# Prefix-attention layer on one core: reciprocals stored by two transfers and spread by four a block, TensorE's order in the loop fixed, picking and divisions queued behind the scan and the Gelu

## The chip, the cores and the metric

The kernel runs on one core of one Trainium2 chip. The metric is device time in microseconds (us): the median of the runs of one launch. Each launch takes the fp32 input `x` of shape (4, 128, 64, 64) and all weights from device memory and writes an output of `x`'s shape there.

## The reference

`x` holds four images of 128 channels and 4096 positions. Layer 0 normalises it by groups, runs three 1x1 convolutions with a PReLU, and adds a softmax attention over the 4096 positions. Layer 1 takes the positions as tokens `t` of 128 numbers and adds two things to them. The first is an attention with one query per head and a running softmax: at each token it is the mean over everything up to that token.

```python
kv = einsum('btd,ed->bte', x, W_kv).reshape(b, t, h, d, 2)   # 8 heads, d = 128
kv = silu(kv)
k, v = kv[..., 0], kv[..., 1]
s = einsum('hd,bthd->bth', q_proj, k)
m_A = cummax(s, axis=1)
exp_scores = exp(s - m_A)
u_A = cumsum(exp_scores, axis=1)
w_A = cumsum(exp_scores[..., None] * v, axis=1)
return (w_A / u_A[..., None]).mean(axis=2)
```

The second is a feed-forward part with 64 experts. Each expert picks its own eight tokens of an image, pools them by their probabilities, and its output goes back to the same tokens.

```python
logits = einsum('bsd,ed->bse', x, gate_w) + gate_b
probs = softmax(logits, axis=1)                      # over the 4096 tokens
vals, idx = top_k(probs.transpose(0, 2, 1), 8)
pooled = einsum('bked,bke->bed', gathered, topv)
h = gelu(einsum('ebd,edh->ebh', [pooled, 1], weight1))
out = einsum('ebh,eho->ebo', [h, 1], weight2)
outputs = zeros.at[flat_idx].add(out * topv)
```

Both parts read `t` normalised over its 128 numbers, and the second sees what the first has added.

## The kernel before

The whole of `t` stays on chip. Layer 0 (about the first 1500 us) ends before layer 1 begins, and the change does not touch it. Everything that follows is layer 1 (`layer1`), which has three parts: the loop over blocks, the tail with the experts, and the output.

**The loop.** The 16384 tokens are cut into 32 blocks of 512 (`NB`, `BLK`), eight (`NBLK`) to an image. Pass n of the loop (L982 on) finishes block n and prepares block n+1; the helpers it calls, each with its line, are these.

- `tokens` (L663): VectorE normalises the block's four chunks of 128 tokens (`xl`, L95). `turned` (L673): TensorE transposes them (`ltr`), ScalarE copies them out (`xt`).
- `keys` (L682): for each of eight heads one matmul `pk` (L687) into a PSUM tile and a Silu on ScalarE (`ks`, L689). The PSUM pool of these tiles has three buffers under the tag "kv"; `pk`, `pe`, `gtr`, `ctr`, `pv`, `pl`, `pp` and `ltr` all take their buffer from it in turn.
- `score` (L702): eight small matmuls give `ps`. `scan` (L712): VectorE copies it in two halves (`ss`), runs the maximum along the tokens (`mm`, L723), subtracts (L727); ScalarE takes the Exp (L728), GpSimd copies it into block order (`es`, L733); VectorE runs the sum (`rr`, L738), keeps the last value (L742), and takes the reciprocal 1/u (L743).
- `spread` (L746): 1/u has to reach all 128 partitions. SyncE stores `rr` to device memory (`rd`, L753) and loads it back, repeated 64 times (`rb`, L761).
- `weights` (L768): TensorE transposes `es` (`pe`, L772), ScalarE copies (`et`, L774), VectorE and GpSimd build `ew` (L779) and the masked `em` (L787). `weighted` (L794): VectorE multiplies `em` by `rb` (L796).
- `values` (L799): matmuls `pv` (L808) and Silus `v` (L812) on ScalarE. `totals` (L816): sums of the eight sub-blocks (`pt`, L824) and eight running sums on VectorE (`before`, L834). `outputs` (L836): TensorE combines all (`po`, L844 and L851), and VectorE adds it to `t` (L856).
- For the experts, a block or two behind: `gate_stats` (mean and variance, VectorE), `gate_norm` (L875: Sqrt on ScalarE, L90; reciprocal `grs` on VectorE, L91; the normalised `xg`, L95, on GpSimd), `gate_turn` (`gtr`, `xt2`), `gate_logits` (matmul `pl`, ScalarE's bias add `lg`, VectorE's best eight `ca`, L904).

**Picking.** For images 0 and 1 (p = 0) the picking is done inside the loop, in passes 18 to 26. `select` (L906) finds on VectorE the eight best of a whole image. Then `pick`, once a pass for eight passes: VectorE's match-replace marks the best in the block's logits (`left`, L930), ScalarE replaces the logits by their Exp (L933), and VectorE clears those that were not marked (L936). One pass later `pick_turn` (`ctr` L943, `ct` L946) and `pick_add` sum the chosen tokens. `divisors` (L971) takes one over the sum of the Exps, once. For images 2 and 3 (p = 1) the same is done in the tail.

**What sets the order.** A planner sorts each engine's instructions by a priority that follows the program's order. `tc.issue_after(x)` puts what is issued in its block behind instruction x on the same engine. In the loop it stands around `weighted`, `gate_norm` and `pick`. [...] SyncE's queue holds the stores and loads of `spread`.

**The tail** (L1032 on) makes the gate of the last two blocks, picks for p = 1, and runs 16 groups of four experts: `first` (`ph` L1099, copy `hr` L1104), `turn` (transposes `htr` L1111, bias add L1115, Gelu L1120), `second` (L1127), `back` (transposing `t` for the output, L1141). One block of Exps is scaled by the divisor per group (`probs`, L1156). Then the experts' outputs (`eo`, L1164) are put back by matmuls (`sct`) and the output is written.

Functions with a second prefix ("g_") belong to a branch that is not executed.

Of the kernel before, what the change touches and what calls it, by code (L numbers as in the profile page):

```python
# [8 lines left out]
F32 = mybir.dt.float32  # L9
AF = mybir.ActivationFunctionType  # L10
# [8 lines left out]
def conv_attn_hybrid_kernel(  # L19
# [22 lines left out]
    nc = tc.nc  # L42
    B, C, N = x.shape
    R = w1t.shape[1]
    NH = qt.shape[1]
# [3 lines left out]
    NCH = N // P  # L49
    BLK = 512  # L50
    NBLK = N // BLK
# [575 lines left out]
    QG = 4  # L627
# [9 lines left out]
    def layer1(pre, ready):  # L637

        with ExitStack() as kept, ExitStack() as l1:
# [72 lines left out]
            def scan(n, pss):  # L712

                k = n % NBLK
                ss = sb.tile([P, BLK], F32, tag="ss", name=f"{pre}ss_{n}", bufs=1)
                for q in range(NPAIR):
                    half = bass.ts(q, BLK // NPAIR)
                    nc.vector.tensor_copy(
                        ss[:, half].rearrange("h (u s j) -> h s u j", u=2, s=2),
                        pss[:, half].rearrange("h (s u j) -> h s u j", u=2, s=2),  # L720
                    )
                mm = sb.tile([P, BLK], F32, tag="mm", name=f"{pre}mm_{n}", bufs=1)
                nc.vector.tensor_tensor_scan(  # L723
                    out=mm, data0=ss, data1=ss, op0=ALU.max, op1=ALU.max,
                    initial=state[:, 0:1] if k else LOWEST,
                )
                nc.vector.tensor_sub(ss, ss, mm)  # L727
                exp = nc.scalar.activation(ss, ss, AF.Exp).ins  # L728
                nc.gpsimd.tensor_copy(state[:, 0:1], mm[:, BLK - 1 : BLK])  # L729
                es = sb.tile([P, BLK], F32, tag="es", name=f"{pre}es_{n}")  # L730
                for q in range(NPAIR):
                    half = bass.ts(q, BLK // NPAIR)
                    nc.gpsimd.tensor_copy(  # L733
                        es[:, half].rearrange("h (s u j) -> h s u j", u=2, s=2),
                        ss[:, half].rearrange("h (u s j) -> h s u j", u=2, s=2),
                    )
                rr = sb.tile([P, BLK], F32, tag="rr", name=f"{pre}rr_{n}")
                nc.vector.tensor_tensor_scan(  # L738
                    out=rr, data0=ones.to_broadcast([P, BLK]), data1=ss,
                    op0=ALU.mult, op1=ALU.add, initial=state[:, 1:2] if k else 0.0,  # L740
                )
                nc.vector.tensor_copy(state[:, 1:2], rr[:, BLK - 1 : BLK])  # L742
                nc.vector.reciprocal(rr, rr)  # L743
                return es, rr, exp

            def spread(n, rr):  # L746

                rd = dram.tile([2, NPAIR, 2, NH, H2], F32, tag="rd", name=f"{pre}rd_{n}")
                by_row = rr.rearrange("(g w) (q u s j) -> w u g q s j", g=QG, q=NPAIR, u=2, s=2)
                for r in range(NR):  # L750
                    for u in range(2):
                        for q in range(NPAIR):
                            nc.sync.dma_start(  # L753
                                out=rd[u, q, :, r * QG : (r + 1) * QG, :].rearrange("s g j -> g s j"),
                                in_=by_row[r, u][:, q],
                            )
                rbs = []
                for q in range(NPAIR):
                    rb = sb.tile([P, 2, NH, H2], F32, tag="rb", name=f"{pre}rb_{n}_{q}")
                    for u in range(2):  # L760
                        nc.sync.dma_start(  # L761
                            out=rb[u * H2 : (u + 1) * H2],
                            in_=rd[u, q].unsqueeze(0).to_broadcast([H2, 2, NH, H2]),
                        )
                    rbs.append(rb)
                return rbs
# [173 lines left out]
            def pick_turn(p, k, ps):  # L940
                ptr = ps.tile([P, CPB, P], F32, tag="kv", name=f"{pre}ctr_{p}_{k}")
                for c in range(CPB):
                    nc.tensor.transpose(ptr[:, c, :], lgs[p][:, bass.ts(k * CPB + c, P)], ident)  # L943
                ct = gp.tile([P, CPB, 2, E], F32, tag="ct", name=f"{pre}ct_{p}_{k}", bufs=2)
                rs = rs1[:, bass.ts(p, 2 * NCH)].rearrange("t (z i) -> t i z", z=2)
                nc.vector.tensor_mul(  # L946
                    ct, ptr.rearrange("t c (z e) -> t c z e", z=2),
                    rs[:, bass.ts(k, CPB), :].unsqueeze(3).to_broadcast([P, CPB, 2, E]),
                )
                cts[p, k] = ct  # L950

            def pick_sum(p, k, pp, start, stop):
                for c in range(CPB):
# [21 lines left out]
            if not ready:  # L975
                for at in range(B * NCH):
                    chunk_stats(gp, mv1[:, at, :], at, f"{pre}st1_{at}")
                roots(rs1, mv1)
            xt = {n: turned(n, tokens(n)) for n in range(2)}
            made = scan(0, score(0, keys(0, xt[0], range(NH))))  # L980
            rbs = spread(0, made[1])
            for n in range(NB):  # L982
                more = n + 1 < NB
                if more:
                    ks = keys(n + 1, xt[n + 1], range(NH // 2))
                if n >= 1:
                    gate_stats(n - 1)
                if n + 2 < NB:
                    xls = tokens(n + 2)
                    xl_last = xls.pop()  # L990
                es, rr, _ = made
                ems = weights(n, es)
                if n >= 2:
                    gate_turn(n - 2, ps_kv)
                if more:
                    ks += keys(n + 1, xt[n + 1], range(NH // 2, NH))
                with tc.issue_after(xl_last):
                    aas = weighted(ems, rbs)
                k0 = n - (B // 2 * NBLK + 2)
                if 1 <= k0 <= NBLK:  # L1000
                    pick_turn(0, k0 - 1, ps_kv)
                vs, last = values(n, xt[n])
                if n >= 2:
                    best = gate_logits(n - 2, ps_kv)
                if 1 <= k0 <= NBLK:
                    pick_add(0, k0 - 1)
                with tc.issue_after(last):
                    if n >= 1:
                        gate_norm(n - 1, nc.gpsimd)
                    if n == 0 and ready:  # L1010
                        roots(rs1[:, bass.ts(B - 1, NCH)], mv1[:, bass.ts(B - 1, NCH), :])
                if n + 2 < NB:
                    xt[n + 2] = turned(n + 2, xls)
                totals(n, vs)
                if more:
                    made = scan(n + 1, score(n + 1, ks))
                    rbs = spread(n + 1, made[1])
                    last = made[2]
                with tc.issue_after(last):
                    if k0 == 0:  # L1020
                        select(0)
                    if 0 <= k0 < NBLK:
                        pick(0, k0)
                    if k0 == NBLK:
                        divisors(0)
                outputs(n, rr, aas, vs)
                if n >= 2:
                    best()
                if n == 0 and ready:
                    test_rows(gp, ps_kv)  # L1030

            l1.close()  # L1032
            pool = opener(l1, pre)
# [28 lines left out]

            gate_stats(NB - 1)
            gate_norm(NB - 1, nc.vector)
            for n in (NB - 2, NB - 1):
                gate_turn(n, ps_a)
                gate_logits(n, ps_a)()
            select(1)
            pp = ps_p.tile([P, C + 1], F32, tag="pp", name=f"{pre}pp_1")
            for k in range(NBLK + 1):  # L1070
# [36 lines left out]
            def turn(g, hr):  # L1107

                ptr = ps_a.tile([P, FC, QG, QW], F32, tag="kv", name=f"{pre}htr_{g}")
                for c in range(FC):  # L1110
                    nc.tensor.transpose(  # L1111
                        ptr[:, c].rearrange("p u b -> p (u b)"), hr[:, bass.ts(c, P)], ident
                    )
                hs = fs.tile([P, FC, QG, QW], F32, tag="hs", name=f"{pre}hs_{g}")
                nc.vector.tensor_tensor(  # L1115
                    hs, ptr,
                    fb1s[:, bass.ts(g, QG), :].rearrange("p u c -> p c u")
                    .unsqueeze(3).to_broadcast([P, FC, QG, QW]), ALU.add,
                )
                nc.scalar.activation(hs, hs, AF.Gelu)  # L1120
                return hs

            def second(g, hs):
                po = ps_p.tile([P, C], F32, tag="po", name=f"{pre}po2_{g}")
# [21 lines left out]

            hr = first(0)
            for g in range(EG):
                hs = turn(g, hr)
                if g + 1 < EG:  # L1150
                    hr = first(g + 1)
                for n in range(g * NB // EG, (g + 1) * NB // EG):
                    back(n)
                p, k = g // NBLK, g % NBLK
                probs = lgs[p][:, bass.ts(k, BLK)]
                nc.scalar.activation(probs, probs, AF.Copy, scale=rden[:, p : p + 1])  # L1156
                second(g, hs)
            eo = []
            for p in range(B // 2):
# [94 lines left out]
```

## Time and profile before

| | us |
|---|---|
| median of 3 runs | 2545.86 |
| lowest and highest | 2544.01, 2548.97 |
| the profiled execution | 2545.14 |
| its span, first to last instruction | 2543.4 |
| layer 1's loop, first scan to last scan | 842.1 |
| tail and output, from the last scan | 187.7 |

The loop's first scan (L723) starts at 1513.60 and its last at 2355.73, both of the span. The page cuts the span into 40 slices of 63.6 us; the loop lies in slices 24 to 37, where TensorE is busy for 90% or more in all but the first:

```
PE   5899999999999999999999989999999999999787
DVE  6677777777776777766666665655656656665624
ACT  2344434444344444444444445565655665666431
POOL 0000000000000000000000002333333333333200
PEclk9999999999999999999999999999999999999898
DMA  3100110000100000000000002111121111112485
```

Each digit is a busy share in tenths. PEclk is the clock granted to TensorE, in tenths of full speed. Groups of instructions that the change touches, with busy time and the mean length of one:

```
L743 DVE RECIPROCAL rr<-rr 128x512 f32<-128x512 f32 x32 | 107.2, 3351 | 0.8
L796 DVE TENSOR_TENSOR em<-em,rb 128x1024 f32<-128x1024 f32 x64 | 78.4, 1226 | 242.4 <-DMA rb<-rd 242.3
L728 ACT ACT_TABLE_LOAD x32 | 41.1, 1283 | 209.3 <-DVE ss L727 209.3
L689 ACT ACTIVATE ks<-pk 128x512 f32<-128x512 f32 x256 | 146.6, 598 | 55.4 <-PE pk L687 55.0
rd<-rr SPq DMA_DIRECT2D x256, 2.0 KB
rb<-rd SPq DMA_DIRECT2D x128, 256.0 KB
```

Behind the bar stand the busy time in us, the mean of one in ns, and the engine's idle time just before these instructions with what ended most of it. The last two are transfers: how many, and the size of each. A table load brings another function (Exp, Silu, Sqrt) into ScalarE.

### The profile page before, as it was taken

The page shows a single profiled execution, that of the slowest core. Times are in us where ns is not written, and L with a number is a line of the kernel's source. Part 1 is how long each engine was busy: PE and PEld are TensorE (multiplying, and loading weights), DVE is VectorE, ACT ScalarE, POOL GpSimd, SP SyncE. Part 2 cuts the span into 40 slices and gives each one's busy share as a digit, 9 for nine tenths or more (in the row PEclk, how much of TensorE's full clock was granted, in tenths as well). Part 3 has the DMA queues.
Part 4 walks back from the last instruction along what each step waited for, and adds up shares of the span by engine and source line. Part 5 has one row for each costly group of instructions (what it writes and reads, how often), then busy time and mean ns, then how long its engine had stood idle before and what let it go on. Part 6 is the DMA issues. An engine that isn't in the chain of part 4 may idle for free.

```text
span 2543.4 us, 45698 instructions
## 1 busy us (share of the span) xinstructions
PE 2406.8 (95%) x19348; PEld 1592.4 (63%) x19348; DVE 1662.0 (65%) x2644; ACT 1182.3 (46%) x1557; POOL 311.6 (12%) x374
## 2 busy tenths in 40 slices
PE   5899999999999999999999989999999999999787
PEld 3567767677677677776777755555555555555543
DVE  6677777777776777766666665655656656665624
ACT  2344434444344444444444445565655665666431
POOL 0000000000000000000000002333333333333200
PEclk9999999999999999999999999999999999999898
DMA  3100110000100000000000002111121111112485
GB/s 96 56 17 12 27 50 9 17 11 24 50 13 5 17 22 17 17 9 9 5 5 9 5 1 52 36 42 46 35 52 36 35 48 40 36 35 52 159 332 210
DMA packets 49063, 111.06 MB, mean 44 GB/s; under 512 B 10960, under 2 KB 19792, under 8 KB 48720
## 3 DMA queue, kind: packets, MB, share of 16 engines
q1 hardware_dynamic: 47552, 107.78, 14.3%
q8 instruction: 153, 2.51, 0.4%
q14 instruction: 62, 0.51, 0.1%
q10 hardware_dynamic: 1296, 0.26, 0.1%
HBM read 86.38 MB, written 8.91 MB: 37 GB/s over the span
## 4 chain that ended last, share of the span: by engine, by line
PE 61%; DVE 19%; DMA 7%; SPq 6%; ACT 3%; issue 2%; ACTq 0%; DVEq 0%; POOL 0%
PE av L494 34%; PE sc L470 17%; DMA rb<-rd 6%; SPq L753 4%; DVE rr L743 4%; DVE before L834 2%; SPq L761 2%; DVE rr L738 2%; ACT L728 2%; DVE mm L723 1%; DVE em L796 1%; PE pa L437 1%; PE ph L1099 1%; PE pd L519 1%; DVE xl L95 1%
## 5 line engine op out<-in xcount | busy, mean ns | idle before, releaser
L494 PE MATMUL av<-pr,am 64*128 64x512 f32 x4096 | 1190.1, 592 | 5.5 <-DVE o L505 5.5
L474 ACT ACTIVATE pr<-sc 128x1024 f32<-128x1024 f32 x512 | 523.9, 1023 | 705.6 <-PE sc L470 695.1
L494 PEld LDWEIGHTS av<-pr,am 64*128 64x128 f32 x4096 | 679.2, 188 | 258.4 <-issue 59.4
L481 DVE TENSOR_TENSOR acc<-acc,pr 128x1024 f32<-128x1024 f32 x480 | 585.4, 1220 | 332.8 <-ACT pr L474 320.8
L470 PE MATMUL sc<-e,e 64*128 64x512 f32 x2048 | 737.1, 594 | 0.0
L470 PEld LDWEIGHTS sc<-e,e 64*128 64x128 f32 x2048 | 351.9, 188 | 102.3 <-issue 29.0
L687 PE MATMUL pk<-xt,wks 128*128 128x512 f32 x512 | 250.3, 624 | 45.2 <-ACT ks L689 40.1
L796 DVE TENSOR_TENSOR em<-em,rb 128x1024 f32<-128x1024 f32 x64 | 78.4, 1226 | 242.4 <-DMA rb<-rd 242.3
L808 PE MATMUL pv<-wvs,xt 128*128 128x512 f32 x512 | 226.0, 594 | 0.0
L687 PEld LDWEIGHTS pk<-xt,wks 128*128 128x128 f32 x512 | 91.9, 194 | 157.4 <-issue 76.8
L812 ACT ACTIVATE v<-pv 128x512 f32<-128x512 f32 x256 | 152.7, 597 | 68.5 <-PE pv L808 68.4
L689 ACT ACTIVATE ks<-pk 128x512 f32<-128x512 f32 x256 | 146.6, 598 | 55.4 <-PE pk L687 55.0
L808 PEld LDWEIGHTS pv<-wvs,xt 128*128 128x128 f32 x512 | 97.1, 191 | 118.7 <-issue 116.3
L728 ACT ACT_TABLE_LOAD x32 | 41.1, 1283 | 209.3 <-DVE ss L727 209.3
L95 POOL TENSOR_SCALAR xg<-t,gmv,grs 128x128 f32<-128x128 f32 x124 | 98.8, 809 | 258.2 <-DVE grs L91 211.9
L695 POOL MEMSET ew<- 128x1024 f32 x1 | 1.0, 951 | 1051.7 <-PE pa L437 1051.7
L844 PEld LDWEIGHTS po<-v,em 64*64 64x64 f32 x4096 | 111.4, 133 | 28.8 <-DVE before L834 10.9
L844 PE MATMUL po<-v,em 64*64 64x128 f32 x4096 | 119.4, 271 | 2.3 <-DVE em L796 2.3
L787 POOL TENSOR_TENSOR em<-et,mask 128x1024 f32<-128x1024 f32 x64 | 120.3, 1901 | 6.4 <-ACT et L774 6.4
L527 DVE RECIPROCAL den<-den 128x512 f32<-128x512 f32 x32 | 107.3, 3353 | 1.1
L743 DVE RECIPROCAL rr<-rr 128x512 f32<-128x512 f32 x32 | 107.2, 3351 | 0.8
L729 POOL COPY state<-mm 128x1 f32<-128x1 f32 x32 | 20.7, 646 | 508.5 <-DVE mm L723 508.3
(164 smaller groups left out, 2275.4 us busy)
## 6 DMA issues: line engine op xcount, KB each, us to landing
rb<-rd SPq DMA_DIRECT2D x128, 256.0 KB
fw<-in_fw_dram SPq DMA_DIRECT2D x64, 512.0 KB
x<-in_x_dram SPq DMA_DIRECT2D x16, 512.0 KB
xr<-in_x_dram SPq DMA_DIRECT2D x32, 256.0 KB
e<-ee SPq DMA_DIRECT2D x64, 128.0 KB
out_dram<-t SPq DMA_DIRECT2D x16, 512.0 KB
e<-ee SPq DMA_DIRECT2D x64, 64.0 KB
rd<-rr SPq DMA_DIRECT2D x256, 2.0 KB
```

Source lines behind the costliest of these rows:

```text
L95: i = engine.tensor_scalar(out=dst, in0=t[:, chunk, :], scalar1=mean, scalar2=rs, op0=ALU.subtract, op1=ALU.mult)
L470: nc.tensor.matmul(sc[:, u, :], e2[halves[u], p, :], e1[halves[u], :], start=True, stop=True)
L474: nc.scalar.activation(pr, sc, AF.Exp)
L481: nc.vector.tensor_add(acc, acc, pr)
L494: nc.tensor.matmul(av, am[h, j, :], pr[h, u, :], start=(j == 0), stop=(j == NCH - 1))
L687: nc.tensor.matmul(pk, wks[:, h, :], xt, start=True, stop=True)
L689: nc.scalar.activation(ks, pk, AF.Silu)
L743: nc.vector.reciprocal(rr, rr)
L787: nc.gpsimd.tensor_tensor(em, eq.unsqueeze(2).to_broadcast([P, 2 * NH, H2]), mask.unsqueeze(1).to_broadcast([P, 2 * NH, H2]), ALU.mult,)
L808: nc.tensor.matmul(pv.rearrange("p h d -> p (h d)"), xt[:, bass.ts(2 * q + s, P)], wvs[:, bass.ts(m, BLK)], start=True, stop=True,)
L812: last = nc.scalar.activation(v[:, bass.ts(m, HPB), :], pv, AF.Silu).ins
L844: nc.tensor.matmul(po[s * H2 : (s + 1) * H2, u, q, :], aas[q][half, s, h, :], vs[2 * q + s][half, h, :], start=(q == 0 and h == 0), stop=F ...
```

## The change

The change has four parts.

1. `spread` stores a block's 1/u in another layout by two transfers of 8 KB, instead of eight of 2 KB. The four loads of 256 KB read this layout. `scan` now also returns its reciprocal instruction.
2. The loop stands in a function that runs with TensorE's order fixed to the program's order. A few calls change place with it: in pass 0 the second half of `keys` comes before `weights`, and the norm, turn and logits of block 30 come into the last pass, with `xg` on VectorE instead of GpSimd.
3. `select`, `pick` and `divisors` are put behind the scan's Exp on ScalarE and behind the scan's reciprocal on VectorE, where they were behind the Exp alone. `weighted`, which was behind the last `xl` of `tokens`, comes behind `pick_turn` in the passes that have one, and has no such edge in the others.
4. In the tail, each group's scaling of `probs` comes behind that group's Gelu on ScalarE.

Of the loop the diff shows the new lines alone; those that they replace are L979 to L1030 above.

```diff
                     op0=ALU.mult, op1=ALU.add, initial=state[:, 1:2] if k else 0.0,
                 )
                 nc.vector.tensor_copy(state[:, 1:2], rr[:, BLK - 1 : BLK])
-                nc.vector.reciprocal(rr, rr)
-                return es, rr, exp
+                inverse = nc.vector.reciprocal(rr, rr).ins
+                return es, rr, (exp, inverse)
             def spread(n, rr):
-                rd = dram.tile([2, NPAIR, 2, NH, H2], F32, tag="rd", name=f"{pre}rd_{n}")
-                by_row = rr.rearrange("(g w) (q u s j) -> w u g q s j", g=QG, q=NPAIR, u=2, s=2)
+                rd = dram.tile([NPAIR, 2, 2, NH, H2], F32, tag="rd", name=f"{pre}rd_{n}")
+                by_row = rr.rearrange("(g w) (c j) -> w g c j", g=QG, j=H2)
                 for r in range(NR):
-                    for u in range(2):
-                        for q in range(NPAIR):
-                            nc.sync.dma_start(
-                                out=rd[u, q, :, r * QG : (r + 1) * QG, :].rearrange("s g j -> g s j"),
-                                in_=by_row[r, u][:, q],
-                            )
+                    nc.sync.dma_start(
+                        out=rd.rearrange("q u s (r g) j -> r g (q u s) j", r=NR)[r], in_=by_row[r]
+                    )
                 rbs = []
                 for q in range(NPAIR):
                     rb = sb.tile([P, 2, NH, H2], F32, tag="rb", name=f"{pre}rb_{n}_{q}")
                     for u in range(2):
                         nc.sync.dma_start(
                             out=rb[u * H2 : (u + 1) * H2],
-                            in_=rd[u, q].unsqueeze(0).to_broadcast([H2, 2, NH, H2]),
+                            in_=rd[q, u].unsqueeze(0).to_broadcast([H2, 2, NH, H2]),
                         )
                     rbs.append(rb)
                 return rbs
...
                     nc.tensor.transpose(ptr[:, c, :], lgs[p][:, bass.ts(k * CPB + c, P)], ident)
                 ct = gp.tile([P, CPB, 2, E], F32, tag="ct", name=f"{pre}ct_{p}_{k}", bufs=2)
                 rs = rs1[:, bass.ts(p, 2 * NCH)].rearrange("t (z i) -> t i z", z=2)
-                nc.vector.tensor_mul(
+                i = nc.vector.tensor_mul(
                     ct, ptr.rearrange("t c (z e) -> t c z e", z=2),
                     rs[:, bass.ts(k, CPB), :].unsqueeze(3).to_broadcast([P, CPB, 2, E]),
                 )
                 cts[p, k] = ct
+                return i.ins
             def pick_sum(p, k, pp, start, stop):
                 for c in range(CPB):
...
                 for at in range(B * NCH):
                     chunk_stats(gp, mv1[:, at, :], at, f"{pre}st1_{at}")
                 roots(rs1, mv1)
...
+            def loop():
+                xt = {n: turned(n, tokens(n)) for n in range(2)}
+                made = scan(0, score(0, keys(0, xt[0], range(NH))))
+                rbs = spread(0, made[1])
+                for n in range(NB):
+                    more = n + 1 < NB
+                    if more:
+                        ks = keys(n + 1, xt[n + 1], range(NH // 2))
+                    if n >= 1:
+                        gate_stats(n - 1)
+                    if not more:
+                        gate_norm(n - 1, nc.vector)
+                    if n + 2 < NB:
+                        xls = tokens(n + 2)
+                    if n == 0:
+                        ks += keys(n + 1, xt[n + 1], range(NH // 2, NH))
+                    es, rr, _ = made
+                    ems = weights(n, es)
+                    if n >= 2:
+                        gate_turn(n - 2, ps_kv)
+                    if more and n > 0:
+                        ks += keys(n + 1, xt[n + 1], range(NH // 2, NH))
+                    k0 = n - (B // 2 * NBLK + 2)
+                    if 1 <= k0 <= NBLK:
+                        with tc.issue_after(pick_turn(0, k0 - 1, ps_kv)):
+                            aas = weighted(ems, rbs)
+                    else:
+                        aas = weighted(ems, rbs)
+                    vs, last = values(n, xt[n])
+                    if n >= 2:
+                        best = gate_logits(n - 2, ps_kv)
+                    if not more:
+                        gate_turn(n - 1, ps_kv)
+                    if 1 <= k0 <= NBLK:
+                        pick_add(0, k0 - 1)
+                    with tc.issue_after(last):
+                        if n >= 1 and more:
+                            gate_norm(n - 1, nc.gpsimd)
+                        if n == 0 and ready:
+                            roots(rs1[:, bass.ts(B - 1, NCH)], mv1[:, bass.ts(B - 1, NCH), :])
+                    if n + 2 < NB:
+                        xt[n + 2] = turned(n + 2, xls)
+                    totals(n, vs)
+                    if not more:
+                        best()
+                        best = gate_logits(n - 1, ps_kv)
+                    if more:
+                        made = scan(n + 1, score(n + 1, ks))
+                        rbs = spread(n + 1, made[1])
+                        with tc.issue_after(made[2][0]), tc.issue_after(made[2][1]):
+                            if k0 == 0:
+                                select(0)
+                            if 0 <= k0 < NBLK:
+                                pick(0, k0)
+                            if k0 == NBLK:
+                                divisors(0)
+                    outputs(n, rr, aas, vs)
+                    if n >= 2:
+                        best()
+                    if n == 0 and ready:
+                        test_rows(gp, ps_kv)
+            with tc.manual_schedule(engines={mybir.EngineType.PE}):
+                loop()
             l1.close()
             pool = opener(l1, pre)
...
             gate_stats(NB - 1)
             gate_norm(NB - 1, nc.vector)
-            for n in (NB - 2, NB - 1):
-                gate_turn(n, ps_a)
-                gate_logits(n, ps_a)()
+            gate_turn(NB - 1, ps_a)
+            gate_logits(NB - 1, ps_a)()
             select(1)
             pp = ps_p.tile([P, C + 1], F32, tag="pp", name=f"{pre}pp_1")
             for k in range(NBLK + 1):
...
                     fb1s[:, bass.ts(g, QG), :].rearrange("p u c -> p c u")
                     .unsqueeze(3).to_broadcast([P, FC, QG, QW]), ALU.add,
                 )
-                nc.scalar.activation(hs, hs, AF.Gelu)
-                return hs
+                return hs, nc.scalar.activation(hs, hs, AF.Gelu).ins
             def second(g, hs):
                 po = ps_p.tile([P, C], F32, tag="po", name=f"{pre}po2_{g}")
...
             hr = first(0)
             for g in range(EG):
-                hs = turn(g, hr)
+                hs, gelu = turn(g, hr)
                 if g + 1 < EG:
                     hr = first(g + 1)
                 for n in range(g * NB // EG, (g + 1) * NB // EG):
                     back(n)
                 p, k = g // NBLK, g % NBLK
                 probs = lgs[p][:, bass.ts(k, BLK)]
-                nc.scalar.activation(probs, probs, AF.Copy, scale=rden[:, p : p + 1])
+                with tc.issue_after(gelu):
+                    nc.scalar.activation(probs, probs, AF.Copy, scale=rden[:, p : p + 1])
                 second(g, hs)
             eo = []
             for p in range(B // 2):
```

## The prediction

> **What bounds the kernel now.** I read first the page's busy shares and the chain that ended last, then the windows view of layer 1 cut at the scan's starts, then TensorE's waits in those windows, and last single turns in the timeline.
>
> ```profile
> PE 2406.8 (95%) x19348; PEld 1592.4 (63%) x19348; DVE 1662.0 (65%) x2644; ACT 1182.3 (46%) x1557; POOL 311.6 (12%) x374
> ...
> PE av L494 34%; PE sc L470 17%; DMA rb<-rd 6%; SPq L753 4%; DVE rr L743 4%; DVE before L834 2%; SPq L761 2%; DVE rr L738 2%; ACT L728 2%; DVE mm L723 1%; DVE em L796 1%; PE pa L437 1%; PE ph L1099 1%; PE pd L519 1%; DVE xl L95 1%
> ```
>
> TensorE is busy for 95% of the span, but `av` and `sc` are layer 0, which the change leaves alone. Layer 1's part of the chain is another thing: stores (L753), loads (L761), `rb<-rd`, reciprocal. So cut it into turns; turn n runs from the scan L723 of block n to that of block n+1.
>
> ```profile
> 1567.62:1967.56 399.94, 377.04 (x5077) 215.13 (x5071) 235.82 (x526) 239.22 (x375) 144.27 (x167) 1.00 0.17 42
> ...
> 2022.96:2251.00 228.04, 218.76 (x2964) 127.95 (x2960) 143.66 (x319) 137.54 (x224) 77.67 (x89) 0.99 0.16 39
> ```
>
> ```profile
> PE pk L687 <- ACT ks L689: 22.5, 14, 2.2
> ```
>
> Columns of the windows: window, length, busy of PE, PEld, DVE, ACT, POOL, then PEclk, DMA share, GB/s. Turns 2 to 16 last 399.94/15 = 26.66 each and TensorE works 377.04/15 = 25.14 of it. The 1.5 between them is one wait a turn (the waits view of turns 2 to 16: 22.5 in all, 14 waits, 2.2 the longest), put down to ScalarE; ScalarE is late because of the chain of one turn:
>
> ```profile
> 1806.99 1.21 DVE mm L723
> ...
> 1812.69 3.35 DVE rr L743
> ...
> 1816.60 0.04 SPq L753
> ...
> 1820.01 0.50 SPq L753
> ...
> 1820.62 0.50 SPq L761
> ...
> 1822.48 5.49 DMA rb<-rd
> ...
> 1828.05 1.23 DVE em L796
> ...
> 1834.10 1.21 DVE mm L723
> ```
>
> From the scan's start: reciprocal ends at +9.13; eight stores issue until 1820.52 and four loads from 1820.62, last byte at 1827.97, 11.93 after the reciprocal; `em` ends at 1829.27; 4.75 of VectorE's small work (`xl`, `grs`, `ca`, six `before` sums, the copies of `ss`) leads to the next scan. VectorE, kept by rb, turns the next tokens late, and ScalarE and TensorE wait for that. So plain turns hang on the spread, by 1.5.
>
> The pick turns 19 to 26 (second window) are TensorE's: 228.04 long, and its waits there add to 0.5 (turn 19), 4.8 (20 to 25) and 4.0 (26). Lengths: 28.01, six of 27.79, 33.29. TensorE's own need is about 26.99.
>
> [...] 8 KB of `eo` landed 1.27 after its issue. [...] after 5.0 of idle at 1541 to 1546:
>
> ```profile
> 1546.00:1547.00 1.00, 0.39 (x1) 0.39 (x2) 1.00 (x5) 0.00 (x0) 0.00 (x0) 0.50 0.00 0
> ...
> 1551.00:1552.00 1.00, 1.00 (x4) 0.48 (x3) 0.48 (x2) 0.23 (x2) 0.44 (x1) 0.50 0.13 51
> ...
> 1553.00:1554.00 1.00, 1.00 (x4) 0.46 (x3) 0.50 (x1) 0.74 (x2) 1.00 (x2) 1.00 1.03 234
> ```
>
> [...] Turn 26 of before shows it: the scaling of L1156 waits 3.88 for a VectorE division, the Silu behind it waits with it, and TensorE loses 3.09:
>
> ```profile
> 2229.21 0.72 ACT L1156 ACTIVATE lg<-lg,rden 128x512 f32<-128x512 f32 x1 [3.88 <-DVE rden L973]
> ...
> 2229.84 0.58 ACT L689 ACTIVATE ks<-pk 128x512 f32<-128x512 f32 x1
> ...
> 2230.47 5.40 PE L687 MATMUL pk<-xt,wks 128*128 128x512 f32 x8 [3.09 <-ACT ks L689]
> ```
>
> **Part 1, the spread.** Eight stores of 2 KB become two of 8 KB; the four loads and their bytes stay. The stores' issue, 8 x 0.55, becomes 2 x 0.52 = 1.05. But the loads now follow their stores so closely that they must wait for the landing: before, none waited (the load of the last store was issued 1.25 after it). I take 1.4; bounds 1.25 (below it a wait would have shown) [...]. The loads themselves took 7.35 from first issue to last byte, at 215 to 240 GB/s, and that stays. So 1.05 + 1.4 + 7.35 = 9.8 instead of 11.93: 2.1 saved [...]. The chain's 26.66 falls to 24.6, under TensorE's 25.14; TensorE is late next, and the gain is cut to 1.5 less some leftover wait, 0.2. Plain turn 25.34.
> Turns 2 to 16: 15 x 25.34 - 399.94 = -19.8. Turn 17: 29.05 to 25.34, -3.7. Turn 18: 26.35, -1.0. Turns 27 to 30: 104.73 against TensorE's 100.8 and 0.4 left over, -3.5.
>
> **Part 2, the picking.** In the instruction order of the changed program, VectorE's match-replace (L930) now stands right behind the reciprocal, and ScalarE's queue in a pick turn reads: Exp of `ss`, Silu table load, `ks_0`, Exp table load, Exp of `lg`, Silu table load, `ks_1` to `ks_7`. Before it read: Exp of `ss`, Exp of `lg`, one Silu load, `ks_0` and on. Exp of `lg` overwrites what the match-replace reads, so it waits for it, and seven Silus queue behind the wait. The prices stand in one pick turn of before:
>
> ```profile
> 2082.68 0.71 ACT L933 ACTIVATE lg<-lg,ng 128x512 f32<-128x512 f32 x1
> ...
> 2083.50 1.28 ACT L689 ACT_TABLE_LOAD   x1
> ...
> 2084.80 1.57 ACT L689 ACTIVATE ks<-pk 128x512 f32<-128x512 f32 x3
> ...
> 2085.16 0.68 DVE L930 MATCH_REPLACE8 left<-ca,lg 128x512 f32<-128x512 f32 x1
> ```
>
> Reciprocal at +9.13 (plain turn: nothing of the picking is ahead of it now), match-replace 0.68 and gaps: +9.90; Exp of `lg` from +9.94; table load and start of `ks_1` 2.12 later (2082.68 to 2084.80): +12.06, ended +12.61. TensorE, whose order is fixed, has behind the last `ps` (1.26 before the scan) `po` with L851 4.67, four `pk` 3.54: ready at +6.95 for `pe`. The PSUM pool "kv" has three buffers, and the one `pe` wants is freed by `ks_1`. Stall: 12.66 - 6.95 = 5.7, with the restart 5.86. The first pick has `select`'s small VectorE work, about 4.1, ahead of its match-replace, but lets `ks_1` and `ks_2` through first: 8.2.
> A wait of that length also drops the clock: before shows 0.50 for one or two windows of 3.4 us behind idles of 3 to 5 us. 3.1 to 6.5 us of work at half speed lose 1.6 to 3.3; I take 2.4 (from 0 to 3.3). A pick turn: 26.99 + 5.86 + 2.4 = 35.25; turn 19: 37.6.
> Turn 19: +9.6. Turns 20 to 25: 6 x 35.25 - 166.74 = +44.8. Turn 26: 33.29 to 35.25, +2.0; it loses the eight scalings and their 3.09 wait, and takes the pick's stall.
> Nothing hides this stall: TensorE is the bound of these turns, and spread's 2 us of slack is no help to it.
>
> **Part 3, the rest.** The scalings of L1156 go behind each group's Gelu, where ScalarE is idle for most of a group's 5.95: nothing. TensorE's fixed order is nearly the one it had; the first turns lose a wait of `pe` for `es`: -1.4. Norm, turn and logits of block 30 move into the last pass: its Sqrt table load and the Silu load after it stand in ScalarE's queue among the `v` activations, and hold TensorE for about 3.2, `po` gets its rb 2.1 earlier, and a Sqrt load of 1.28 comes onto the tail's path; with small waits +3.5 (0 to 6). In the tail one `gtr` and `pl` go, covered there.
>
> **Sum.** -19.8 - 3.7 - 1.0 + 9.6 + 44.8 + 2.0 - 3.5 - 1.4 + 3.5 = +30.5. The profiled execution took 2545.14 (span 2543.4), 0.7 under the runs' median of 2545.86. Predicted 2576. With x for what a pick turn has over TensorE's 26.99, the sum is 8x - 38: it breaks even at x = 4.7; mine is 8.55. Without the clock's share x is 6.15, still slower. About 5 us, 0.2%, is what a measurement can tell from no change.
>
> **Rivals.**
> A, main, 0.70: as above, 2576; 2562 to 2590 from the clock's 1.6 to 3.3, the last pass and the landing.
> B, 0.12: the spread gains a third of that, because [...] the loads are bound by their megabyte. Plain turns 26.3: 17 x 0.96 more, 2592. For: the loads fill 5.5 of 11.9. Against: the 4.4 of issue that goes stood on the chain in full.
> C, 0.09: stall without a clock drop (x = 6.15): 8 x 6.15 - 38 = +11, 2557. [...] Against: turn 26 of before, where 3.09 of idle was followed by 3.2 at 0.50.
> D, the other side, 0.09: the match-replace is ready when ScalarE gets to its Exp, so that only ScalarE's own two loads and Exp count, 2 x 1.28 + 0.71 less TensorE's slack: x = 3.0[...]; -14, 2532. It decides below x = 4.7, that is if `ks_1` ends 1.2 earlier against TensorE than I have it and the clock holds. For: all of +6.95 is pieced together from other turns. Against: the 3.35 reciprocal stands ahead of the match-replace in VectorE's order, and in before the match-replace was ready only because it stood ahead.
>
> Slower 0.88, within 0.2% 0.02, faster 0.10. The range reaches from C to B: 2555 to 2594.
>
> **What will show it.** TensorE waits for ScalarE's `ks` before `pe`, 5 to 6 us each in seven turns and about 8 in turn 19, with PEclk of 0.50 behind each; ScalarE's L933 Exp waits for the match-replace, with a table load on both sides. Scan to scan: 25.3 in turns 2 to 16, 35 in 20 to 25. Two stores a block[...], and a chain through layer 1 that runs over TensorE. I am wrong if pick turns stay under 31.7, or if plain turns stay above 26.

## The result, and the profile after

| | before | after |
|---|---|---|
| median, us (4 runs each) | 2545.81 | 2558.73 |
| lowest and highest | 2544.01, 2548.97 | 2557.49, 2560.27 |
| profiled execution's span | 2543.4 | 2555.8 |

The changed kernel is slower by 12.9 us: ratio 1.005, 95% interval 1.0032 to 1.0067. Slower was forecast, but 30 us were expected, more than twice as much. In the spans the difference is 12.4.

The page of the changed kernel, busy shares and chain:

```profile
PE 2412.5 (94%) x19348; PEld 1598.9 (63%) x19348; DVE 1677.5 (66%) x2648; ACT 1206.8 (47%) x1575; POOL 310.0 (12%) x370
...
PE 84%; DVE 9%; ACT 3%; DMA 2%; issue 1%; SPq 0%; ACTq 0%; DVEq 0%
```

Before, TensorE had 61% of that chain, DMA 7% and SyncE's queue 6%. The spread has all but left the path: outside the pick turns the chain of the loop now runs over TensorE, and `rb<-rd` has 1.6% of it in turns 2 to 16, where it had 19.4% before. The windows view shows turns 2 to 16 (the first line) and the pick turns 19 to 26 (the second):

```profile
1563.27:1935.68 372.41, 372.35 (x5035) 212.94 (x5029) 236.58 (x526) 239.41 (x375) 144.47 (x167) 1.00 0.19 45
...
1985.45:2262.09 276.64, 231.68 (x2964) 136.98 (x2956) 158.76 (x330) 155.38 (x232) 79.96 (x89) 0.90 0.14 32
```

The first stretch took 399.94 before and takes 372.41, with TensorE busy in all of it. The second took 228.04 and takes 276.64. The waits view of TensorE in the second stretch has almost all of what came on top (us in all, how many, longest):

```profile
PE pe L769 <- ACT ks L689: 38.0, 7, 5.5
PE pk L687 <- ACT ks L689: 7.0, 1, 7.0
```

TensorE stood idle for 45.0 us. One such turn in the timeline (turn 21, scan at 2056.62):

```profile
2061.96 0.60 ACT L689 ACTIVATE ks<-pk 128x512 f32<-128x512 f32 x1
...
2062.40 3.35 DVE L743 RECIPROCAL rr<-rr 128x512 f32<-128x512 f32 x1
2062.57 1.28 ACT L930 ACT_TABLE_LOAD   x1
...
2065.69 0.67 DVE L927 MATCH_REPLACE8 left<-ca,lg 128x512 f32<-128x512 f32 x1
...
2066.40 0.72 ACT L930 ACTIVATE lg<-lg,ng 128x512 f32<-128x512 f32 x1 [2.54 <-DVE left L927]
...
2067.23 1.28 ACT L689 ACT_TABLE_LOAD   x1
...
2068.52 1.57 ACT L689 ACTIVATE ks<-pk 128x512 f32<-128x512 f32 x3
2069.26 1.09 PE L769 MATMUL pe<-ident,es 128*128 128x128 f32 x4 [5.47 <-ACT ks L689]
```

Read it from below. `pe` has stood 5.47 for a buffer that `ks_1` frees; `ks_1` stood behind a table load, the Exp of `lg`, and the table load ahead of that; the Exp stood 2.54 for the match-replace, which came behind the 3.35 of the reciprocal. The windows view over the same turn shows what became of TensorE's clock (last column but two):

```profile
2066.00:2067.00 1.00, 0.00 (x0) 0.00 (x0) 1.00 (x3) 0.60 (x1) 0.00 (x0) 0.95 0.00 0
2068.00:2069.00 1.00, 0.00 (x0) 0.00 (x0) 0.80 (x4) 0.99 (x2) 0.56 (x1) 0.50 0.00 0
2072.00:2073.00 1.00, 1.00 (x3) 0.48 (x2) 0.61 (x1) 0.05 (x1) 1.00 (x2) 0.50 1.11 246
2073.00:2074.00 1.00, 1.00 (x2) 0.32 (x2) 0.00 (x0) 0.55 (x1) 1.00 (x1) 0.64 0.82 180
2074.00:2075.00 1.00, 1.00 (x4) 0.44 (x3) 0.00 (x0) 0.60 (x1) 0.43 (x1) 1.00 0.05 8
```

The clock was at half from about 2066.9 to 2073.7, and TensorE's first 4.4 us of work fall into it. Where the 12.4 of the spans come from, with the prediction's terms beside them:

| stretch | predicted | measured |
|---|---|---|
| to the first scan, and turns 0 and 1 | -1.4 | -4.4 |
| turns 2 to 16 | -19.8 | -27.5 |
| turns 17 and 18 | -4.7 | -5.6 |
| turn 19 | +9.6 | +8.3 |
| turns 20 to 25 | +44.8 | +39.4 |
| turn 26 | +2.0 | +0.9 |
| turns 27 to 30 | -3.5 | -4.9 |
| from the last scan on | +3.5 | +6.2 |
| sum | +30.5 | +12.4 |

Of the first row, 1.2 lies ahead of the first scan, mostly in layer 0, which the change leaves alone. The first scan starts anywhere from 1511.1 to 1513.8 in the thirteen kernels, so that part says nothing of the change. Of turn 17's gain of 4.1, the spread brings 1.6 (27.46 in e1 below). The other 2.5 comes with the pick's edge: with the spread alone `select` and the first match-replace stood at 1959 to 1962, ahead of the next scan at 1964.68; in the changed kernel they stand in turn 19.

### The profile page after: what moved, and what is told of

Read it like the earlier page. It is cut to its first block, busy times and chain, and to the rows that moved or that the text cites. A ratio compares the mean times of both kernels' runs of the same rounds, so it can differ in the third digit from the quotient of the medians.

```text
span 2555.8 us, 45522 instructions
## 1 busy us (share of the span) xinstructions
PE 2412.5 (94%) x19348; PEld 1598.9 (63%) x19348; DVE 1677.5 (66%) x2648; ACT 1206.8 (47%) x1575; POOL 310.0 (12%) x370
## 4 chain that ended last, share of the span: by engine, by line
PE 84%; DVE 9%; ACT 3%; DMA 2%; issue 1%; SPq 0%; ACTq 0%; DVEq 0%
PE av L494 33%; PE sc L470 17%; PE pv L805 8%; PE pk L687 8%; PE po L841 3%; PE pt L821 2%; DVE rr L743 2%; PE ps L706 1%; PE pa L437 1%; PE ph L1108 1%; PE pd L519 1%; DVE before L831 1%; PE pp L955 1%; PE pe L415 1%; PE pl L896 1%
```

## The experiments

Each run's ratio is against the kernel before, measured beside it (its median moved between 2545.1 and 2546.9). The changed kernel was timed in the first group alone, so a difference from it carries an uncertainty of 1 to 2 us.

**The spread alone (e1_spread).** On the kernel before, `spread` as in the change and nothing else; TensorE's order stays as it was.

```diff
-                    for u in range(2):
-                        for q in range(NPAIR):
-                            nc.sync.dma_start(
-                                out=rd[u, q, :, r * QG : (r + 1) * QG, :].rearrange("s g j -> g s j"),
-                                in_=by_row[r, u][:, q],
-                            )
+                    nc.sync.dma_start(
+                        out=rd.rearrange("q u s (r g) j -> r g (q u s) j", r=NR)[r], in_=by_row[r]
+                    )
```

> The kernel before with the new spread alone (two stores of 8 KB a block, loads from the new layout); TensorE's order is the one of before. Theory 'spread' (the store issue stood on the chain, and TensorE is next): plain turns fall from 26.66 to 24.8 to 25.1, the pick turns 20 to 25 from 27.8 to about 27.2, turn 26 stays near 33; in all some -33 to -36 us, about 2511. Rival 'order' (the fixed order of TensorE brought the plain turns down to 24.8): plain turns stay at 25.3 or more, and at most -25 us. Rival 'bytes' (the loads bound it): under -8 us.

2504.29, ratio 0.9827 (0.981 to 0.9844): 42.5 us faster, more than either theory gave. The windows view, turns 2 to 16:

```profile
1564.94:1937.22 372.28, 372.25 (x5032) 212.89 (x5026) 236.39 (x526) 239.40 (x375) 143.46 (x167) 1.00 0.19 45
```

That is 24.82 a turn with TensorE full, the same as in the changed kernel, though TensorE's order is that of before. So the gain of the plain turns is the spread's, and 'order' falls. Turns 0 and 1 become 2.8 shorter as well, and turns 20 to 25 fall from 27.79 to about 27.36.

**The pick as before (e2_pick_old).** The changed kernel with one edge less.

```diff
-                        with tc.issue_after(made[2][0]), tc.issue_after(made[2][1]):
+                        with tc.issue_after(made[2][0]):
```

> The changed kernel with the pick behind the scan's Exp alone again, so that VectorE has the match-replace ahead of the reciprocal and ScalarE the Exp of the logits directly behind the scan's Exp, as before the change. Theory 'queue' (the pick's place makes the stall): TensorE's waits before pe, 45 us in turns 19 to 26, go, and PEclk stays at 1.0 there; pick turns fall from 34.3 to about 27; 50 to 58 us faster than the changed kernel, 2501 to 2509. Rival 'fixed order' (the stall comes from TensorE's order being fixed, with pe where the scan's chain is latest): the waits before pe stay over 3 us a turn and the time over 2530.

2501.57, ratio 0.9816 (0.9798 to 0.9833): 57.2 us below the changed kernel. Turns 19 to 26:

```profile
1989.52:2208.34 218.82, 215.81 (x2968) 127.30 (x2963) 144.29 (x322) 133.34 (x216) 77.77 (x89) 1.00 0.17 41
```

The clock is 1.00 throughout and TensorE's waits are down to 3.0 in all. This also takes the loss of 57.8 in these turns apart. 42.0 of it is more standing. The other 15.9, or 2.0 a turn, is busy time: the same work takes 215.81 here and 231.68 in the changed kernel. That is put down to half clock, and a separate count gives the same size: in the changed kernel TensorE is busy for 34.6 us, over all stretches of these turns with its clock at half, and half of that is 17.3. The moved edge of `weighted` has no run of its own; e1 has the old one and e2 the new one, and turns 20 to 25 last 27.35 in both.

**The pick's edge alone (e3_pick_only).** On the kernel before: `pick` behind the reciprocal too, eight stores, planner's order.

```diff
-                with tc.issue_after(last):
+                with tc.issue_after(last[0]), tc.issue_after(last[1]):
                     if k0 == 0:
                         select(0)
```

> The kernel before with the pick behind the reciprocal alone; spread with its eight stores, TensorE's order left to the planner. Theory 'queue': ScalarE's queue is that of the changed kernel in the pick turns (two more table loads, the Exp behind the match-replace), TensorE waits 5 to 6 us before pe in each, with PEclk 0.5 behind: turns 20 to 25 go from 27.8 to about 34.3, turn 19 to 36; turn 26 goes to about 38, as it keeps the eight scalings; +50 us, about 2596. Rival 'fixed order': the planner's order hides most of it, pick turns under 31, less than +20 us.

2602.64, ratio 1.0212 (1.0194 to 1.023): 55.9 us slower. Turn 19 is 36.77 and turns 20 to 25 average 35.59. Turn 26 is 35.03 rather than the 38 expected; turn 27 is 3.0 longer than before instead (29.65). So the edge does the damage without the spread and without the fixed order too.

**The loads without the wait (e4_loads_no_wait).** The Exp writes to a tile of its own, so nothing makes it wait for the match-replace; an edge keeps it behind `ks_0`, with both table loads (`keys` calls it, as `between`, after its first Silu).

```diff
+                ex = lg if p else sb.tile([P, BLK], F32, tag="ex", name=f"{pre}ex_{k}", bufs=1)
...
-                    lg, lg, AF.Exp, bias=picks[p], accum_out=den[:, p, k : k + 1]
+                    ex, lg, AF.Exp, bias=picks[p], accum_out=den[:, p, k : k + 1]
...
-                    out=lg, in0=left, scalar=-3.3e38, in1=lg, op0=ALU.is_le, op1=ALU.mult
+                    out=lg, in0=left, scalar=-3.3e38, in1=ex, op0=ALU.is_le, op1=ALU.mult
...
+                    if between:
+                        with tc.issue_after(first):
+                            between()
```

> The changed kernel with the Exp of the logits written to a tile of its own, so that it no longer waits for the match-replace that reads the logits; its place in ScalarE's queue stays behind ks_0, with a table load on both sides. Theory 'wait': the 2.54 us that this Exp waited go, TensorE's stall falls from 5.47 to about 2.9 a turn; with the clock's loss unchanged turns 20 to 25 take 31.8 and the whole 2538, with no clock drop left 29.8 and 2522. Rival 'loads' (the two table loads and the Exp alone fill the stall, the wait lies beside them): the stall stays above 5 us and the time within 5 us of 2558.7.

2533.8, ratio 0.994 (0.9921 to 0.9958), 25 us below the changed kernel. TensorE's waits in turns 21 to 23 (three, so 2.9 each):

```profile
PE pe L773 <- ACT ks L689: 8.8, 3, 2.9
```

'Wait' was right: of the 5.47 that TensorE stood, 2.54 was the wait and 2.9 the two loads and the Exp. The windows view of these three turns shows more:

```profile
2052.30:2082.20 29.90, 26.96 (x382) 15.93 (x378) 18.15 (x41) 19.33 (x29) 10.02 (x11) 1.00 0.15 38
2082.20:2113.50 31.30, 28.36 (x382) 17.11 (x374) 18.05 (x42) 19.44 (x29) 10.02 (x11) 0.95 0.15 36
2113.50:2146.20 32.70, 29.76 (x378) 17.44 (x374) 17.93 (x42) 19.44 (x29) 10.01 (x11) 0.90 0.14 34
```

The same 2.9 of idle costs nothing more, 1.4 more, or 2.8 more: TensorE is busy for 26.96, 28.36 and 29.76. The mean clocks of 1.00, 0.95 and 0.90 agree with 0, 3.4 and 6.8 us at half clock. The trace of the changed kernel has such stretches too: 6.83 us at half clock in each of turns 19 to 26, behind idles of 5.1 to 7.0. Here an idle of 2.9 was followed by half clock in two of the three turns.

**A tile of its own, free in its place (e5_own_tile).** As e4, without the edge behind `ks_0`: the planner puts the Exp right behind the scan's Exp in seven of eight pick turns.

> The changed kernel with the Exp of the logits in a tile of its own and free in its place: it stands right behind the scan's Exp in seven of the eight pick turns (the first still waits for select), without table loads of its own, while the match-replace stays behind the reciprocal. Theory 'queue' (only what stands in ScalarE's queue ahead of ks_1 costs): turns 20 to 26 fall from 34.3 to about 27.0 with no clock drop, turn 19 stays at 34; 51 us off, about 2507. Rival 'reciprocal' (a match-replace behind the reciprocal is itself late, for the clearing and the transposes ctr): turns 20 to 26 stay above 28.5.

2507.65, ratio 0.9841 (0.9826 to 0.9856). Turns 20 to 26 average 27.38, and turn 19 takes 34.3, as its Exp still waits for `select`. In turns 20 to 26 the match-replace stands behind the reciprocal as in the changed kernel, and it costs nothing there: e2, with the match-replace ahead of the reciprocal, has 27.35 a turn in turns 19 to 26. What costs is ScalarE's queue.

**The gate of block 30 back in the tail (e6_gate_tail).** The changed kernel without the calls that came into the last pass.

```diff
-                    if not more:
-                        gate_norm(n - 1, nc.vector)
...
-                    if not more:
-                        gate_turn(n - 1, ps_kv)
...
+            for n in (NB - 2, NB - 1):
+                gate_turn(n, ps_a)
+                gate_logits(n, ps_a)()
```

> The changed kernel with norm, turn and logits of block 30 back in the tail and its xg on GpSimd. Theory 'last pass' (the Sqrt load, the Silu load behind it and the late gate of block 31 cost what the stretch after the last scan gained, 6.2 us): 3 to 6 us off, 2553 to 2556, and the last output matmul of the loop ends 24.3 us after the last scan, not 27.5. Rival 'chance' [...]: within 2 us of 2558.7.

2551.27 against 2558.73, 7.5 us off and more than the 3 to 6 expected; ratio 1.0019 (1.0012 to 1.0026). The loop's last addition to `t` (L853) starts 28.6 us after the last scan in the changed kernel, 23.0 here. ScalarE in the changed kernel's last pass:

```profile
2371.28 0.60 ACT L809 ACTIVATE v<-pv 128x512 f32<-128x512 f32 x1
2371.89 1.28 ACT L90 ACT_TABLE_LOAD   x1
2373.84 0.30 ACT L90 ACTIVATE grs<-gmv,eps 128x4 f32<-128x4 f32 x1 [0.67 <-DVE gmv L87]
2374.16 1.28 ACT L809 ACT_TABLE_LOAD   x1
```

Two loads, a wait and a Sqrt stand in the middle of the `v`, and TensorE waits 2.6 for the next buffer (`pv`).

**TensorE's order left to the planner (e7_planner_order).** The changed kernel, with `loop()` called without the fixed order.

```diff
-            with tc.manual_schedule(engines={mybir.EngineType.PE}):
-                loop()
+            loop()
```

> The changed kernel with TensorE's order left to the planner. Theory 'no part' (the fixed order moves a few matmuls only, the stall and the gain of the plain turns are the same without it): pick turns 34.3, plain turns 24.8, within 3 us of 2558.7. Rival 'order pays': plain turns back above 25, at least 4 us slower. Rival 'order costs': the stall before pe under 4 us, at least 12 us faster.

2565.53, ratio 1.0073 (1.0059 to 1.0087): 6.8 us above the changed kernel, so 'no part' fails. Yet 'order pays' isn't right as put: the plain turns stay at 24.81. The difference lies in turns 19 to 26, 284.7 against 276.6. In most of these turns TensorE's wait before `pe` is shorter (4.5), but its busy time is longer. Turn 23 shows why; the first three lines are of e7, the last is of the changed kernel:

```profile
2137.05 1.05 PE L706 MATMUL ps<-ks,qz 128*32 128x512 f32 x2
2143.29 1.92 PE L706 MATMUL ps<-ks,qz 128*32 128x512 f32 x2
2161.94 1.91 PE L706 MATMUL ps<-ks,qz 128*32 128x512 f32 x12
2156.59 1.92 PE L706 MATMUL ps<-ks,qz 128*32 128x512 f32 x16
```

In the changed kernel the 16 `ps` of a block stand together and take 1.92. The planner draws two pairs out of them, one ahead of `pe` and one behind it. The 12 that stay take as long as the 16 did, and the pairs come on top: 1.05 inside the wait, and 1.92 behind it, at half clock. The kernel before has the 16 together in turns 19 to 25; e3, with the pick's edge and the planner's order, has the same pairs. So the 6.8 is what the fixed order saves once the pick stalls, not something it gains over the kernel before.

**The scalings behind the Gelu (e8_scale_later).** On the kernel before, this edge alone.

```diff
-                nc.scalar.activation(probs, probs, AF.Copy, scale=rden[:, p : p + 1])
+                with tc.issue_after(gelu):
+                    nc.scalar.activation(probs, probs, AF.Copy, scale=rden[:, p : p + 1])
```

> The kernel before with the scaling of each block's probabilities behind its group's Gelu alone. Theory 'queue': the scaling that waited 3.88 us for the division no longer stands ahead of the Silus in turn 26, which falls from 33.3 to about 27.8; the tail hides the eight scalings; 5.5 us off, about 2540.5. Rival 'tail': the eight scalings more in the tail delay the groups, less than 2 us off.

2541.63, ratio 0.998 (0.9971 to 0.9989): 5.2 us off, as 'queue' had it. Turn 26 falls from 33.29 to 28.41, and the stretch from the last scan on stays as long (187.4, 187.6 before).

**Four stores (e9_four_stores).** The changed kernel with four stores of 4 KB.

```diff
                 for r in range(NR):
-                    nc.sync.dma_start(
-                        out=rd.rearrange("q u s (r g) j -> r g (q u s) j", r=NR)[r], in_=by_row[r]
-                    )
+                    for q in range(NPAIR):
+                        nc.sync.dma_start(
+                            out=rd.rearrange("q u s (r g) j -> r q g (u s) j", r=NR)[r, q],
+                            in_=by_row[r][:, 4 * q : 4 * q + 4],
+                        )
```

> The changed kernel with four stores of 4 KB a block where it has two of 8 KB: some 1.1 us more of issue on the way to rb, and nothing else. It asks what the plain turns hang on after the change. Theory 'TensorE' (its 24.8 a turn is the bound, and the chain has slack): turns 2 to 16 rise by less than 0.4 each, the whole by less than 8 us. Rival 'chain' (scan, stores, loads and em still set the turn, and TensorE only looks full): turns 2 to 16 rise by about 1.0 each, 18 to 22 us in all. Turns 19 to 26 stay at 34.3 in both, as the stall ends later than rb.

2562.61, 3.9 us above the changed kernel; turns 2 to 16 rise by 0.19 each. That is within what 'TensorE' allowed, but the run says less than it was meant to. Four stores take 2.25 to issue where two took 1.16, yet the first load follows the first store by 2.90 instead of 2.45 on average, so only some 0.45 of the 1.1 reaches rb. More than half of that is hidden, and TensorE waits again for 1.1 in all in these turns. So the plain turns hang on TensorE, as its 372.35 of 372.41 in the changed kernel says too, and the spread's slack is small, some 0.3 a turn.

**Two versions that beat both (e10_select_early, e11_pick_old_gate_tail).** e11 joins the edits of e2 and e6. e10 has e6, the Exp of e5, and `select` one scan earlier:

```diff
                     ems = weights(n, es)
+                    if n == B // 2 * NBLK + 2:
+                        with tc.issue_after(made[2][1]):
+                            select(0)
```

> The changed kernel with three edits: the Exp of the logits in a tile of its own and free to stand right behind the scan's Exp; select one scan earlier, behind the reciprocal of that scan, so that the first pick waits for nothing either; the gate of block 30 back in the tail. Theory 'queue': no stall is left in turns 17 to 26, turn 19 falls to 27.4 like the others, turn 17 stays at 24.95 and turn 18 near 24.9; about 2494, 52 us below the kernel before, and below every other run. Rival 'VectorE' (eight small operations of select more in turn 18 delay ew and the sums): turn 18 rises by 1.5 or more, about 2497.

> The changed kernel with the pick behind the scan's Exp alone, as before the change, and the gate of block 30 back in the tail. Theory 'queue' and theory 'last pass' add up: 2501.6 less 3 to 7.5 us, 2494 to 2498, with turn 17 at 27.7 and turns 19 to 26 at 27.4. Rival: the last pass costs nothing where the clock falls otherwise, 2501.

e10: 2496.98, ratio 0.9809 (0.9796 to 0.9823); turn 17 is 24.95, turn 18 is 24.68, turns 19 to 26 are 27.36 each. e11: 2496.69, ratio 0.981 (0.9796 to 0.9823); turn 17 is 27.46. In the loop e10 gains what was expected of it; in the profiled executions its stretch from the last scan on is 3 us longer, with a lower mean clock (0.89 against 0.92), and the two come out level. Both are 48 us below the kernel before. Against e2, moving the gate gives e11 4.9 us, less than the 7.5 of e6.

## Why the prediction was wrong in size

The mechanism was right, in sign and place; the sizes of two terms were not. Rival A happened, though the time lies below A's own 2562 to 2590. B fell with e1, C fell since the clock dropped in every pick turn (6.83 us at half clock in each), and D fell with the 5.5 of standing. It is chance that the time comes out next to C's 2557: the clock did drop, and the spread gained more. The forecast was the difference of two large sums: gains of 29.4 and losses of 59.9 in the table above. Measured, the gains are 42.4 and the losses 54.8. The terms:

**Part 1's last step, the plain turn of 25.34, is the largest miss.** The chain was right. The timeline of turn 10 (scan at 1761.03) has stores and loads 2.43 apart, where 1.05 + 1.4 was worked out, the 1.4 being the author's estimate:

```profile
1770.19 1.16 SPq L751 DMA_DIRECT2D rd<-rr  x2
...
1772.62 2.41 SPq L758 DMA_DIRECT2D rb<-rd  x4
...
1779.87 1.23 DVE L793 TENSOR_TENSOR em<-em,rb 128x1024 f32<-128x1024 f32 x1 [1.01 <-DMA rb<-rd]
```

The second `em` starts 18.84 after the scan; 9.13 + 9.8 = 18.9 was said. What failed is "TensorE's 25.14" and the 0.2 of leftover wait: e1, with the order of before, does the same work in 24.82, and no wait is left over. That is 0.5 a turn: 7.7 in turns 2 to 16, and 2.3 in turns 17, 18 and 27 to 30. The 25.14 was TensorE's busy time in the stretch before, divided by 15, and that holds more than the work of 15 turns. The stretch was cut at VectorE's scans, and 5077 matmuls fell into it, where e1's has 5032. And one turn lost its clock. Cut where TensorE's own turn begins (its first `ps`), the kernel before has, in two neighbouring turns and at the wait in the second:

```profile
1855.58:1882.41 26.83, 24.94 (x339) 14.16 (x335) 15.60 (x36) 16.06 (x26) 9.47 (x11) 1.00 0.18 42
1882.41:1911.05 28.64, 26.46 (x339) 15.12 (x335) 17.86 (x42) 16.16 (x26) 9.48 (x11) 0.94 0.16 39
...
1893.96 2.08 PE L687 MATMUL pk<-xt,wks 128*128 128x512 f32 x2 [2.18 <-ACT ks L689]
...
1893.80:1897.20 3.40, 3.24 (x9) 2.10 (x10) 3.40 (x2) 1.88 (x5) 0.00 (x0) 0.51 0.00 0
```

Fourteen of the fifteen turns have 24.68 to 25.01 of work, one has 26.46. In e1 the same turns have 24.67 to 24.95. So 25.14 was about 0.3 too high: some 0.1 each from the cut and from the turn at half clock, and the rest is not explained.

**Part 2's 35.25 measured 34.35.** The stall was 5.47 at most in turns 20 to 26 (5.86 said) and the clock's share 2.0 (2.4 said). The base of 26.99 held: 26.96 in the turn of e4 that kept its clock. Turn 19 was 36.3, not 37.6, with a stall of 7.0 where 8.2 was said. Over the eight turns that makes 7.8. The prediction also held that without the clock's share the kernel would still be slower. By an estimate from these runs it would not: 12.4 less the 15.9 put down to half clock is -3.5, so the sign hung on the clock. No run takes the clock's drop away alone.

**Part 3.** Turns 0 and 1 were given to the fixed order (-1.4); e1 shows that the spread brings 2.8 there. The last pass was put at +3.5, measured +6.2 in the spans, and the gate's move by itself costs 7.5 (e6). The earlier rb gives back some 2 of that in the last pass, as said: the loop's last addition to `t` starts 2.3 us earlier in e6 than before. The whole stretch from the last scan on is as long in e6 as before, though (187.6 both), so the tail lost it again. The scalings in the tail cost nothing, as said: e8 keeps its 5.2.

Do the parts make the whole? From the kernel before to e1 the spread brings -42.5. From e1 to e2 all the rest but the pick's edge brings -2.7. From e2 to the changed kernel the pick's edge brings +57.2. That sums to +12.0, of 12.9 measured. The -2.7 is less well understood: scalings (-5.2) and gate (+7.5) alone would give +2.3.

## What to carry to other kernels

Before putting an instruction behind another engine's late work, look at what stands behind it in its own queue; here an Exp that nobody needed soon held seven Silus that TensorE needed at once. A tile of its own took away its wait of 2.54 us but not the two table loads of 1.28 each (e4); directly behind another Exp it cost nothing (27.35 a turn in e2, 27.38 in e5, against 34.35). Before a busy time is taken as an engine's need, cut the stretch where that engine's own turn begins, and look at the clock turn by turn; here 25.14 stood for 24.8, and a gain cut off at it looked too small. Where a change joins a large gain and a large loss, forecast and try each alone: the spread by itself gave 42.5 us, and the sum hid it.

## What was not expected of the hardware

In the loops of the kernel before and of the changed kernel, half clock came in stretches of 3.41 or 6.83 us. The same idle of 2.9 us cost 0, 1.4 or 2.8 us more, at mean clocks of 1.00, 0.95 and 0.90 (e4). So an idle of this length had no single price here, and in one turn it cost almost as much again as the idle itself. A shorter one cost too: in turns 2 to 16 of the kernel before the longest wait, 2.18, was followed by 3.41 us at half clock and some 1.5 more of work (26.46 against 24.94 in the turn before it), and the others, up to 1.93, by none.

Four `ps` fewer in a group of 16 (128x32 weights, 512 columns) saved nothing: 12 took 1.91 us and 16 took 1.92, while two alone took 1.05 (e7). Here these matmuls were cheap only beside their like.
